# Both ends of a two-layer graph network: denominators in place, other PSUM banks for the last steps, other times and places for the side work

## The chip, the cores and the metric

One core of one Trainium2 chip at a time: the first four experiments (head only, tail only, checks early, all three repairs) ran on one chip and the other seven on another, each group beside its own runs of the kernel before. The engines go by the profile's names: PE is TensorE, DVE VectorE, ACT ScalarE, POOL GpSimd, SP SyncE, which sends most of the DMAs here. PSUM, where TensorE's results land, is shared out in named tiles (`s`, `x`, `qz`, `po`, `pd`). The metric is the device time of one execution in microseconds (us), as the median of several runs. All runs told of here are of the fast state (granted clock 0.993 to 0.996 over the span in the profiled runs), so they can be compared with each other. Of the kernel before, 130 runs were made beside the experiments, and they lie between 3556.3 and 3564.1 us: a difference of 1 us means nothing unless many runs carry it.

## The reference, cut to what matters

```python
# layer 0: pre-norm attention with 8 heads and an adjacency mask; x is 32 x 512 x 512
h = maximum(layernorm(x), 0)
scores = q @ k.T / sqrt(64) + (1 - adj) * -1e9          # q, k, v = h @ Wq, h @ Wk, h @ Wv
x = x + softmax(scores) @ v @ Wo + bo
# layer 1: graph attention
h = maximum(layernorm(x), 0)
hw = h @ W;  s1, s2 = hw @ a1, hw @ a2
att = softmax(leaky_relu(s1[:, None] + s2[None, :]) * adj)
x = x + elu(att @ hw + beta * hw)
```

## The kernel before

One step per batch element b (32, with two more to drain the pipeline). A step has four units of two heads each: scores, exponentials, sums over keys (`es`), denominators (`pd`), values (`po`). Large products are made of seven pieces (names `x_`, `qz_`, `y_`, with the weight combined beforehand), so that sums of operands, made on DVE and POOL, stand between the products. `hn` is the normed input of layer 1, `at` its unnormalised attention matrix, `as` the sum of its four tiles, `pg` the gather `at @ hn`, `dmax` a check of the diagonal.

The order on each engine is the order of the program, and the program decides it with its own clocks: work that is not urgent is put on a list with a time from which it may start, a time by which it is wanted, and a cost. It is taken up where it fits beside TensorE's next piece.

```python
    def pe(us):
        clock["pe"] += us
        till = clock["pe"] + (1.0 if at_ends[0] else 0.4)
        ...   # of the list: what fits until then, the one wanted soonest first
    def later(key, wait, by, cost, fn):
        now = max(clock["dve"], clock["pe"])
        spare.append((key, now + wait, cost, fn, now + by))
    def need(key):
        ...   # everything under this key, now, in order
```

Side work of the first steps: the dot products of W with a (one row per half of W, sent through DRAM to all partitions), W's own combination on POOL, and four checks of adj (`bad`).

```python
        def dot(g, c, o, ar):
            ...   # one multiply-and-sum over 256 columns on DVE
            if c == C - 1 and o == 1:
                ...
                as_row((wa1_r, wa2_r)[g], wa[:, g, :], f"wa{g}")   # by DMA: 512 scattered words
                if g == 1:
                    combine(nc.gpsimd, w1, aw)                      # five operations on POOL
```

Denominators: normally 1/pd goes from PSUM to SBUF on DVE, through DRAM to all partitions, and POOL multiplies. Only the very last unit did it in place in PSUM:

```python
    def finish(b, j, st):
        need("rd")
        if (b, j) == (B - 1, NP - 1):
            return finish_last(b, j, st)
        ...
        def divide():
            nc.vector.reciprocal(rq, pd)
            then("rd", spread)         # ACT copies and sends, SP fetches, POOL multiplies
```

## Time and profile before

| | before |
|---|---|
| median time | 3560.97 us (3559.75 to 3561.69) |
| TensorE (PE) busy | 3506.1 of 3559.0 us |
| TensorE idle before 200 us | 17.5 us |
| TensorE idle after 3400 us | 33.9 us |

The prediction below shows the stretches and the waits. Here are the stretch it leaves out and the places of TensorE's timeline on which both ends are measured. First the stretch from 200 to 400 us (length, then busy PE, PE's weight loads, DVE, ACT, POOL, each with its count, then clock, DMA share, GB/s), then the timeline (start us, busy us, engine, line, operation, out<-in, shapes, count; in brackets the idle time before it and what ended it).

```profile
200.00:400.00 200.00, 199.35 (x1503) 105.90 (x1500) 153.22 (x227) 78.01 (x125) 76.89 (x60) 1.00 0.13 40
```

```profile
152.50 2.08 PE L558 MATMUL ps<-qT,kT 64*128 64x512 f32 x4 [8.48 <-DVE e L570]
...
191.32 1.95 PE L53 MATMUL x_k<-hT,wk 128*64 128x256 f32 x16
...
219.86 3.70 PE L558 MATMUL ps<-qT,kT 64*128 64x512 f32 x16
...
3428.46 3.70 PE L558 MATMUL ps<-qT,kT 64*128 64x512 f32 x16
...
3478.97 1.18 PE L53 MATMUL pe<-ones,as 128*64 128x64 f32 x16 [1.80 <-DVE x L709]
...
3521.06 15.76 PE L53 MATMUL pg<-at,hn 128*64 128x512 f32 x64 [5.52 <-DVE dmax L827]
```

What the reader is to see: from 220 us on TensorE hardly waits (0.65 us idle between 200 and 400), so what the first steps save or lose arrives at the scores of the last unit (3428.46). In twelve of the thirteen traces of this record these two places lie 3207.8 to 3209.4 us apart; the thirteenth is told below. I therefore measure the head by the start of step 2's first scores (219.86) and the tail by the time from the scores of the last unit to the start of the last gather: 3521.06 - 3428.46 = 92.6 us.

### The profile page before, as it was taken

The page shows a single profiled execution, that of the slowest core. Times are in us where ns is not written, and L with a number is a line of the kernel's source. Part 1 is how long each engine was busy: PE and PEld are TensorE (multiplying, and loading weights), DVE is VectorE, ACT ScalarE, POOL GpSimd, SP SyncE. Part 2 cuts the span into 40 slices and gives each one's busy share as a digit, 9 for nine tenths or more (in the row PEclk, how much of TensorE's full clock was granted, in tenths as well). Part 3 has the DMA queues.
Part 4 walks back from the last instruction along what each step waited for, and adds up shares of the span by engine and source line. Part 5 has one row for each costly group of instructions (what it writes and reads, how often), then busy time and mean ns, then how long its engine had stood idle before and what let it go on. Part 6 is the DMA issues. An engine that isn't in the chain of part 4 may idle for free.

```text
span 3559.0 us, 64141 instructions
## 1 busy us (share of the span) xinstructions
PE 3506.1 (99%) x26353; PEld 1885.4 (53%) x26354; DVE 2727.3 (77%) x4207; ACT 1452.9 (41%) x2310; POOL 1396.6 (39%) x1095
## 2 busy tenths in 40 slices
PE   9899999999999999999999999999999999999987
PEld 5455555555555555555555555555555555555544
DVE  6877777787777777777877777877777877778775
ACT  3244443444343444434444434444344444344432
POOL 5332444333443334443334433344433344333342
PEclk9999999999999999999999999999999999999998
DMA  4001111011111011110111110111110111111110
GB/s 137 19 28 49 49 45 46 26 44 45 52 46 37 28 49 48 48 49 31 34 46 51 45 37 30 46 49 48 48 37 28 45 51 46 37 34 43 48 34 28
DMA packets 109395, 154.76 MB, mean 43 GB/s; under 512 B 16492, under 2 KB 54888, under 8 KB 109096
## 3 DMA queue, kind: packets, MB, share of 16 engines
q1 hardware_dynamic: 106496, 148.22, 13.1%
q8 instruction: 210, 3.44, 0.4%
q10 hardware_dynamic: 2392, 2.10, 0.2%
q14 instruction: 89, 0.73, 0.1%
q0 software_dynamic: 208, 0.27, 0.0%
HBM read 116.40 MB, written 34.14 MB: 42 GB/s over the span
## 4 chain that ended last, share of the span: by engine, by line
PE 94%; DVE 4%; DMA 1%; POOL 0%; issue 0%; ACT 0%; SPq 0%; POOLq 0%; ACTq 0%; DVEq 0%
PE ps L558 12%; PE pg L53 12%; PE po L609 12%; PE qz_k L53 5%; PE qz_q L53 5%; PE qz_v L53 5%; PE qz_w L53 4%; PE qz_y L53 4%; PE x_k L53 3%; PE x_v L53 3%; PE x_q L53 3%; PE y_k L53 3%; PE y_v L53 3%; PE y_q L53 3%; PE x_w L53 3%; PE y_w L53 3%
## 5 line engine op out<-in xcount | busy, mean ns | idle before, releaser
L585 ACT ACTIVATE e<-e 128x1024 f32<-128x1024 f32 x512 | 541.5, 1058 | 212.9 <-DVE e L570 176.8
L648 POOL TENSOR_TENSOR oT<-oT,rd 128x512 f32<-128x512 f32 x127 | 172.6, 1359 | 940.7 <-DMA rd<-rd 737.9
L570 DVE SCALAR_TENSOR_TENSOR e<-maskT,ps 128x1024 f32<-128x1024 uint8 x384 | 456.4, 1216 | 85.4 <-PE ps L558 85.2
L558 PE MATMUL ps<-qT,kT 64*128 64x512 f32 x2048 | 478.1, 604 | 12.7 <-DVE e L570 11.6
L609 PE MATMUL po<-e,v 128*64 128x512 f32 x2048 | 464.1, 594 | 0.0
L53 PE MATMUL pg<-at,hn 128*64 128x512 f32 x2048 | 448.9, 596 | 6.3 <-DVE dmax L827 5.5
L582 DVE TENSOR_TENSOR es<-es,e 128x1024 f32<-128x1024 f32 x254 | 381.8, 1503 | 11.0 <-DVE es L582 0.5
L558 PEld LDWEIGHTS ps<-qT,kT 64*128 64x128 f32 x2048 | 186.0, 186 | 301.5 <-issue 206.5
L501 POOL TENSOR_TENSOR qT<-qT,edge 128x256 f32<-128x256 f32 x128 | 85.3, 689 | 560.5 <-DVE qT L497 560.5
L53 PEld LDWEIGHTS pg<-at,hn 128*64 128x64 f32 x2048 | 145.9, 138 | 294.5 <-issue 289.5
L609 PEld LDWEIGHTS po<-e,v 128*64 128x64 f32 x2048 | 148.6, 137 | 229.8 <-issue 217.9
L861 POOL TENSOR_TENSOR y<-y,x 128x512 f32<-128x512 f32 (+1 forms) x126 | 159.5, 1271 | 186.8 <-DVE y L853 183.7
L688 POOL TENSOR_TENSOR x<-x,c_row 128x512 f32<-128x512 f32 x128 | 193.3, 1530 | 98.9 <-DMA x<-in_x_dram 98.9
L359 DVE TENSOR_SCALAR x<-x,mv,rs 128x512 f32<-128x512 f32 x128 | 103.5, 851 | 158.7 <-POOL rs L334 158.5
L638 DVE RECIPROCAL rd<-pd 128x256 f32<-128x256 f32 x127 | 222.3, 1750 | 2.7 <-POOL oT L648 2.3
L793 ACT ACTIVATE at<-at 128x512 f32<-128x512 f32 x128 | 80.2, 628 | 290.3 <-DVE at L789 286.2
L766 DVE CUSTOM_DVE_ANT_0 scr<-hn,wa_r 128x512 f32<-128x512 f32 x256 | 168.8, 689 | 36.7 <-ACT hn L753 36.7
L582 DVE TENSOR_TENSOR es<-e,e 128x1024 f32<-128x1024 f32 x127 | 189.7, 1494 | 0.9 <-PE pd L629 0.8
L53 PE MATMUL qz_y<-w,vT 128*64 128x256 f32 x1520 | 182.8, 383 | 5.2 <-ACT qz_y L464 3.0
L851 DVE TENSOR_SCALAR y<-y 128x512 f32<-128x512 f32 x128 | 56.2, 439 | 142.3 <-ACT y L848 142.3
L565 DVE SCALAR_TENSOR_TENSOR e<-maskT,ps 128x512 f32<-128x512 uint8 x256 | 163.6, 680 | 0.0
L839 ACT COPY gT<-pg 128x512 f32<-128x512 f32 x128 | 74.9, 586 | 197.8 <-PE pg L53 195.9
(228 smaller groups left out, 6315.0 us busy)
## 6 DMA issues: line engine op xcount, KB each, us to landing
x<-in_x_dram SPq DMA_DIRECT2D x130, 256.0 KB
out_dram<-y SPq DMA_DIRECT2D x128, 256.0 KB
rd<-rd SPq DMA_DIRECT2D x254, 128.0 KB
x<-in_x_dram SPq DMA_DIRECT2D x62, 512.0 KB
s<-row_s SPq DMA_DIRECT2D x32, 256.0 KB
rd<-rd ACTq DMA_DIRECT2D x127, 4.0 KB
adj<-in_adj_dram SPq DMA_DIRECT2D x4, 256.0 KB
wk<-in_L_gnn_Wk_dram ACTq DMA_DIRECT2D x3, 256.0 KB
```

The source lines that it names most:

```text
L53: nc.tensor.matmul(out[s : s + HD], lhsT[:, s : s + HD], rhs, start=start, stop=stop, skip_group_check=onto)
L558: nc.tensor.matmul(ps[s], st["kT"][j][rows, ts(k, P)], st["qT"][j][rows, :], start=True, stop=True)
L565: nc.vector.scalar_tensor_tensor(e[:, s, :], maskT[:, k, :], NEG, ps[s], op0=ALU.mult, op1=ALU.add)
L570: nc.vector.scalar_tensor_tensor(e, maskT[:, k, :].unsqueeze(1).to_broadcast([P, 2, N]), NEG, p, op0=ALU.mult, op1=ALU.add)
L582: (nc.gpsimd if early else nc.vector).tensor_tensor(es, one, e, op=ALU.add)
L585: nc.scalar.activation(e, e, AF.Exp)
L609: nc.tensor.matmul(po[s * HD : (s + 1) * HD, :], v[k // 2][:, k % 2, (2 * j + s) * HD : (2 * j + s + 1) * HD], e[k][:, s, :], start=k == 0 ...
L638: nc.vector.reciprocal(rq, pd)
L648: then("rd", lambda: nc.gpsimd.tensor_tensor(o, o, rd, op=ALU.mult), 6.0)
L688: nc.gpsimd.tensor_tensor(r[:, t, :], r[:, t, :], c_row, op=ALU.add)
L766: nc.vector.tensor_tensor_reduce(scr, st["hn"][t], r, 1.0, 0.0, op0=ALU.mult, op1=ALU.add, accum_out=st["s12"][:, g, t : t + 1],)
L861: (nc.vector if b == B - 2 else nc.gpsimd).tensor_tensor(yu, yu, x_[:, :, ts(i, H)], op=ALU.add)
```

## The change

Its intent: at the head, get DVE's dot products and checks out of the way of the scores (the wait of 8.48 us); at the tail, free PSUM banks and get DVE sooner through its list. Cut to its core:

```diff
-            later("bad", 60.0, 200.0, 1.35, lambda t=t: other(t))
+            later("bad", 120.0, 200.0, 1.35, lambda t=t: other(t))
...
-                    later("wa", 40.0, 75.0, 0.5, ...dot...)
+                    later("wa", 40.0, 50.0, 0.75, ...dot...)
...      # sums: the longer cost for the third unit in the first two steps too
-                    "es", ..., 1.9 if j == 2 and b > 1 else 1.2,
+                    "es", ..., 1.9 if j == 2 else 1.2,
...      # where the dots must be done: second half of the first norm, not the first Wo
         def second():
+            need("wa")
...
         def most_of_w():
-            need("wa")
--- tail
-        if (b, j) == (B - 1, NP - 1):
+        if b == B - 1 and j >= NP - 2:
             return finish_last(b, j, st)
...
-        pd = psum.tile([P, N], F32, name=f"pd_{b}_{j}", tag="pd")
+        pd = psum.tile([P, N], F32, name=f"pd_{b}_{j}", tag=("pd", "po")[j % 2])
...      # the pair of the last Wo
+        return seven(f"w{b}", wo, ..., "s" if b == B - 1 else "qz")
...      # the last diagonal: bank po in place of x, and ahead of the elu
-            "P": most_of_y, "E": lambda: diagonal(b - 1, prev), "S": lambda: z_(b - 2),
+            "P": most_of_y, "E": lambda: diagonal(b - 1, prev, "po"), "S": rest_of_y,
...      # k: the last norm's rest and the reciprocals first
-            B: "0p.qmURzviDlngPES", B + 1: "gJY",
+            B: "k0pq.mURzviDlngPES", B + 1: "gJY",
```

The three numbers of `later` are the wait until the work may start, the time by which it is wanted, and its cost. So the checks may start only from 120 us, while the dots are wanted sooner (50 in place of 75 us) at a higher cost each; what comes later for the dots is the place where they must be done. The expectations below call both "wanted later".

Cut are `rest_of_y` (the order of the held elu blocks: block (1,1), then (0,0), then (0,1)), the helper behind `k`, and a start of 16 in place of 4.5 us for `at` of the last two elements. In the last order string the point (the denominators' step) also moved, to behind `q`.

More of the change, by code (lines that the diff above doesn't have):

```diff
@@ L323, in row_constants @@
                 for o in range(2):
-                    later("wa", 40.0, 75.0, 0.5, lambda g=g, c=c, o=o, ar=ar: dot(g, c, o, ar))
+                    later("wa", 40.0, 50.0, 0.75, lambda g=g, c=c, o=o, ar=ar: dot(g, c, o, ar))
     def stats(src, name, mv):
@@ L429, in turn, with seven @@
         st["h"] = h
-    def seven(name, w, B, tokens, one, two, scale=1.0, more=None):
+    def seven(name, w, B, tokens, one, two, scale=1.0, more=None, pair_="qz"):
         def times(p, a, bl, start, onto=False):
@@ L454, in seven @@
         yield
-        qz = psum.tile([P, 2, N], F32, name=f"qz_{name}", tag="qz")
+        qz = psum.tile([P, 2, N], F32, name=f"qz_{name}", tag=pair_)
         z_ = qz[:, 1, :]
@@ L589, in rest @@
                 held.append(lambda: later(
-                    "es", 2.2 if k < T - 1 and b > 1 else 1.2, gap(b, j) - 6.0 + k, 1.9 if j == 2 and b > 1 else 1.2,
+                    "es", 2.2 if k < T - 1 and b > 1 else 1.2, gap(b, j) - 6.0 + k, 1.9 if j == 2 else 1.2,
                     lambda: total(k, e)
@@ L669, in finish_last @@
         finished.add((b, j))
-        st["largest"] = lambda: nc.scalar.activation(
+        st["largest"].append(lambda: nc.scalar.activation(
             pd, pd, AF.Copy, accum_out=rsum[:, b, j : j + 1]
-        )
+        ))
         for k in range(2):
@@ L728, in more @@
             st["share"] = lambda: share(0)
-        return seven(f"w{b}", wo, st["oT"], True, one, two, 1.0 / VS, more)
+        return seven(f"w{b}", wo, st["oT"], True, one, two, 1.0 / VS, more, "s" if b == B - 1 else "qz")
     def norm1(b, st, rows):
@@ L804, in logits, with diagonal @@
         for k in range(T):
-            later(("at", b), 4.5, 20.0, 1.5, lambda k=k: start(k))
-    def diagonal(b, st):
+            later(("at", b), 4.5 if b < B - 2 else 16.0, 20.0, 1.5, lambda k=k: start(k))
+    def diagonal(b, st, tag="x"):
         need(("hn", b))
         need(("at", b))
-        pd = psum.tile([P, T, HD], F32, name=f"pe_{b}", tag="x")
+        pd = psum.tile([P, T, HD], F32, name=f"pe_{b}", tag=tag)
         for t in range(T):
@@ L868, in one, with add @@
         def one(i, k, p):
-            elu(i, k, p)
+            if b == B - 2 and i == 0:
+                st["elu"] = [lambda: elu(i, k, p)]
+            else:
+                elu(i, k, p)
         def two(i, k, p, q):
+            if b == B - 2:
+                st["elu"].append(lambda: add(i, k, p, q))
+            else:
+                add(i, k, p, q)
+        def add(i, k, p, q):
             s = p if i == 0 else wtile([P, N], f"yq_{b}_{i}_{k}", "y", 3)
@@ L885, in new_state @@
             "x": load(b), "e": [[] for _ in range(NP)], "es": {}, "o": [], "x1": [], "at": [], "g": [],
-            "dots": 0,
+            "dots": 0, "largest": [],
         }
@@ L951, in most_of_y, with rest_of_y, last_sums_behind @@
                 next(old["pieces"])
+        def rest_of_y():
+            block0, *others = old["elu"]
+            others[0]()
+            block0()
+            others[1]()
+            z_(b - 2)
+        def last_sums_behind():
+            while any(e[0] == ("hn", b - 2) for e in spare):
+                run_spare(next(i for i, e in enumerate(spare) if e[0] == ("hn", b - 2)))
+            run_all("rd")
         def X():
@@ L1014, in step @@
             "Q": lambda: run(proj_q(b + 1, nxt)),
-            "p": lambda: first_y(b - 3), "q": lambda: more_y(b - 3), "v": lambda: prev["largest"](),
-            "m": lambda: run_all(("hn", b - 2)),
+            "p": lambda: first_y(b - 3), "q": lambda: more_y(b - 3), "v": lambda: [f() for f in prev["largest"]],
+            "m": lambda: run_all(("hn", b - 2)), "k": last_sums_behind,
             "i": most_of_w, "l": lambda: run(prev["pieces"]),
-            "P": most_of_y, "E": lambda: diagonal(b - 1, prev), "S": lambda: z_(b - 2),
+            "P": most_of_y, "E": lambda: diagonal(b - 1, prev, "po"), "S": rest_of_y,
             "f": lambda: residual(b, cur, 0, "x", 4),
```

## The prediction

> **What bounds the kernel now.** I read the page's busy line first, then the stretches of 200 us, then the waits of TensorE (PE) alone, then the timelines of all engines at both ends.
>
> ```profile
> PE 3506.1 (99%) x26353; PEld 1885.4 (53%) x26354; DVE 2727.3 (77%) x4207; ACT 1452.9 (41%) x2310; POOL 1396.6 (39%) x1095
> ...
> 0.00:200.00 200.00, 182.54 (x1443) 104.09 (x1446) 155.96 (x222) 72.32 (x108) 91.43 (x80) 0.97 0.25 76
> ...
> 400.00:600.00 200.00, 200.00 (x1500) 107.07 (x1498) 150.58 (x242) 84.12 (x136) 74.93 (x59) 1.00 0.11 37
> ...
> 3400.00:3600.00 200.00, 125.10 (x848) 64.30 (x844) 100.33 (x185) 46.76 (x83) 57.31 (x48) 0.92 0.08 26
> ```
> The columns of a stretch are its length, then busy PE, weight loads, DVE, ACT, POOL, then clock and DMA. PE is idle 3559.0 - 3506.1 = 52.9 us in all: 17.5 before 200 us and 33.9 of the last 159. The middle is PE without gaps, so a change at the ends can win some 50 us at the very most, 1.4%.
>
> ```profile
> PE ps L558 <- DVE e L570: 11.6, 6, 8.5
> PE qz_w L53 <- DVE y L853: 5.8, 1, 5.8
> PE pg L53 <- DVE dmax L827: 5.5, 1, 5.5
> PE qz_y L53 <- ACT qz_y L464: 3.0, 1, 3.0
> PE pe L53 <- DVE y L853: 2.8, 1, 2.8
> PE qz_w L53 <- ACT qz_w L464: 2.4, 1, 2.4
> PE pd L658 <- ACT pd L644: 2.2, 1, 2.2
> PE qz_y L53 <- DVE yq L874: 2.1, 1, 2.1
> PE pe L53 <- DVE x L709: 1.8, 1, 1.8
> ```
> These are the waits (total us, times, longest) that the change aims at. The 8.5 is one wait at 144 us: the scores' PSUM pair cannot be refilled while DVE works through eleven dots of W with a. From the row "PE qz_w <- DVE y" on, all but the 2.4 lie after 3436 us.
>
> ```profile
> 3447.19 1.22 DVE L748 SCALAR_TENSOR_TENSOR nb<-mv,rs 128x2 f32<-128x2 f32 x1 [3.71 <-POOL rs L334]
> ...
> 3466.36 0.77 DVE L786 SCALAR_TENSOR_TENSOR at<-s,s,adjT 128x512 f32<-128x512 f32 x1
> ...
> 3519.28 1.50 DVE L819 SCALAR_TENSOR_TENSOR at<-ident,bd,at 128x128 f32<-128x128 f32 x4
> ```
> In the timeline of DVE (start, us, idle before it in brackets) from 3434 to 3480 there is one gap worth the name, these 3.71 us: POOL stood with the product of unit 2, waiting for reciprocals to return by DMA, and the 0.7 us power behind it held DVE. So most PE waits at the end are DVE's order, not missing PSUM: what counts there is how much earlier DVE gets through its list.
>
> **What the Trainium skill says.** "TensorE: Matmul & The Clock Gate", What's actually happening: after about 3.4 us of idle window the array runs at half rate until it has again been busy that long. The trace agrees roughly: after the 8.48 us wait four score matmuls took 2.08 us instead of 1.13, and a piece of sixteen that takes 1.73 took 3.68 for 16 after the 5.75 us wait; the clock of 150 to 160 us was 0.71. "SBUF — State Buffer", Who interferes with whom: a DVE operation with two SBUF inputs and a POOL operation that reads SBUF block each other. The trace agrees: the dots took 1.40 us each while POOL was busy and 0.34 when it was not. "DMA: Bandwidth & Descriptors", Queues, rings and completion order: a semaphore increment lands only after every earlier write of that DMA engine, across queues. The trace fits: the row of W·a (512 scattered words) took 10.87 us from issue to release, and the reciprocals' row, sent by ACT at 163.33, released SP only at 169.2. "VectorE: DVE Perf Modes", First, the fixed hardware budget, says that reciprocal iterates; here 128x256 take 1.75 us against 0.69 for a 128x512 product.
>
> **The tail, part by part.** (a) Unit 2's sums in place: one reciprocal of 1.75 becomes two, and a product of 0.69 moves from POOL to DVE: +2.44 on DVE. Against it go the gap of 3.71, the stretched 1.22 us operation behind it (-1.1) and 0.28 of gap at the reciprocal between the dots. (b) The new order on DVE starts with statistics and both nb at 3434.2 to 3436.2, then reciprocals to 3439.6, the product to 3440.3, three sums of 1.22 to 3444.0 (about 0.9 more as POOL's vT falls beside them), eight dots of 0.615 to 3449.8, reciprocals and product to 3453.9. Before, that point was 3455.1: 1.2 gained, and I allow 1.5. (c) PE's wait for the pd bank disappears, but pd_3 now waits for the sums: about 2.3 to 3 us in place of 2.24. The 3.0 for ACT goes, as nb_0 is early, yet PE then waits for yq at 3455 to 3456, some 5 us: DVE is the bound. (d) Last Wo in the scores' banks: the 5.75 wait disappears, Wo's second piece comes 6 us earlier, the third waits for ACT's copy to about 3465. But the next PE instruction that matters, the diagonal of 30, waits for DVE's at and x adds (11.6 us of DVE after the elu). That is moved only by the 1.5 of (b). Most of the 5.75 turns up there again.
> (e) The last diagonal. Before: as ready at 3509.94, then DVE elu work to 3519.03, diagonal to 3521.06, then the gather. After: PE's pe runs as soon as as is there (1.2), DVE's diagonal 2.0, so 3513.2; but the gather's first bank, x, still holds elu block (0,0), now after block (1,1): yq 0.65, exponentials 0.95, 0.44 + 0.88 + 0.67 for (1,1), 0.44 + 0.88 for (0,0) = 4.9 with gaps, so 3518.3. That is 2.7 gained of the 5.5, as the wait passes from dmax to the x bank. Sum: 1.5 + 2.7 = 4.2, plus some 0.6 since the gather (15.76 us against 13.95 of the one at 245 us) starts less cold. Tail: 4.8 gained. From the gather's start to the end nothing changes.
>
> **The head.** (f) Removed: 8.48 + 2.35 (copy behind the reciprocal) + 0.56 (the bad checks before step 1) + about 1.6 (two smaller waits), and some 3 us of slow matmuls: 16. Four dots now precede the scores of unit 1, seven follow, and POOL is idle there, as the combine of W has moved behind a later product. So at the end of the transposes (183.75 before) PE should be some 11.5 us early. (g) That is given back in three places, seen in the order of instructions. First, rd_0's reciprocal is now behind all of e_2, so the bank of pd_1 is free only at 168.2 when PE is there at 164: 4.2 (already in the 11.5). Second, POOL has the product with rd_0, then W's combine (five operations, 5.7), then the power, then tT: the product waits for reciprocals by DMA, queued just behind the second row of W·a. If that row takes 8.4 us as the first did, POOL starts at about 177, t1 is ready at 187.6, and PE, through with x_k at 180.5, waits 7 us (only 3 if the row does not hold it). Third, the four bad checks (1.4 each) stand between the dots and the sums: from the last kT to the qT that frees z DVE has 3.7 + 5.8 + 3.6 + 1.75 + 0.8 + 1.4 + 0.8 = 17.8, plus 0.8 for kT itself, PE 12.7 of work: 5.9 of wait. Two cold starts cost 1.5 each (estimate, from the 1.7 to 2.0 us of the slow pieces above). From the end of x_k, which was at 193.3 and would now be at 180.5: 12.8 - 7.1 - 1.5 - 5.9 - 1.5 = -3.2. Head: -3, with 4 either way.
> Sum: 4.8 - 3 = 1.8. I lean a little further to a gain, because my chains take every order at its worst: 3.5 us from 3561 gives 3557.5.
>
> **The rivals.** First, *the head keeps its gain*: the combine falls in a gap, the checks run while PE still has projections; then head +8, tail +5: 3548. For it: the 8.48 is one clear wait. Against it: POOL and DVE both work in order, and PE had no slack at 190 to 217 us in the trace. Second, *the tail gives nothing*: POOL operations beside DVE stretch the sums and at by a few us (at L789 0.69 to 1.65 in the trace), head -3: 3564. Third, *all targeted waits vanish*: 8.5 + 5.8 + 5.5 + 3 + 2.8 + 2.4 + 2.2 with their cold matmuls, about 35: 3526. Against it: DVE's list from 3434 to 3480 is full, and the waits hang in one chain.
>
> **Range and chances.** 3557.5 us, with 3549 to 3565 for 8 in 10: the head's three give-backs carry most of the spread. Two per cent would be 71 us, more than PE's whole idle time, so a gain above 2% is out, and a loss needs a stall that nothing shows: 0.005, 0.985, 0.01.
>
> **What would show it.** Right: the 8.5 at 144 us gone, in its place waits for pd_1 (ACT pd, about 4), qz_k (POOL tT, 3 to 7) and qz_q (DVE qT, about 6) between 160 and 220 us; step 2's first scores at 217 to 224 us, against 219.86; in the tail no wait of qz_w for y, a larger wait at pe of 30, the gather of 31 waiting for y L854 in place of dmax, and the last 38 us as before. Wrong: if step 2's scores come before 213 us (the give-backs were not there), or if the gather of 31 starts less than 2 or more than 8 us earlier relative to the start of the last step.

## The result, and the profile after

| | before | after |
|---|---|---|
| median time | 3560.97 us | 3561.17 us (3559.06 to 3564.23) |
| ratio, fast runs of the same rounds | 1 | 1.0002, 95% interval 0.9984 to 1.0019 |
| step 2's first scores | 219.86 | 224.80 |
| scores of the last unit | 3428.46 | 3434.01 |
| last gather, counted from there | 92.6 | 89.3 |

A ratio is always the mean time of one kernel's fast runs over that of the other's of the same rounds, so it is not quite the ratio of the medians. The time did not change: 3557.5 had been predicted, with 3549 to 3565 as the range. Below the sum it is not quiet: the head lost 5 us and the tail won 3 to 4. Busy line, stretches and the waits of TensorE of the kernel after:

```profile
PE 3507.7 (98%) x26349; PEld 1887.9 (53%) x26350; DVE 2719.2 (76%) x4209; ACT 1453.1 (41%) x2310; POOL 1390.3 (39%) x1094
```

```profile
0.00:200.00 200.00, 186.36 (x1483) 108.06 (x1484) 141.40 (x211) 73.01 (x109) 86.69 (x81) 0.97 0.23 76
200.00:400.00 200.00, 191.94 (x1414) 100.22 (x1408) 155.82 (x234) 77.56 (x125) 70.73 (x57) 0.98 0.12 39
...
3400.00:3600.00 200.00, 130.35 (x870) 67.13 (x866) 107.16 (x189) 48.09 (x86) 62.93 (x51) 0.92 0.08 25
```

```profile
PE qz_q L53 <- ACT qz_q L464: 6.8, 1, 6.8
...
PE pe L53 <- DVE x L709: 5.1, 1, 5.1
PE qz_k L53 <- POOL hT L379: 4.9, 1, 4.9
PE pd L629 <- ACT pd L644: 4.4, 1, 4.4
...
PE pg L53 <- DVE y L854: 0.8, 1, 0.8
```

TensorE's idle time went down by 3.8 us before 200 us and up by 7.4 between 200 and 400 us: the 8.5 at 144 us is gone, and three waits (4.4, 4.9, 6.8) stand in its place further on. The 5.8 of Wo and the 5.5 of the gather are gone too; the first is largely back as 5.1 at the diagonal of element 30. The places in TensorE's timeline that answer to those of before:

```profile
187.47 3.57 PE L53 MATMUL qz_k<-hT,wk 128*64 128x256 f32 x16 [4.86 <-POOL hT L379]
...
214.06 3.68 PE L53 MATMUL qz_q<-tT,wq 128*64 128x256 f32 x16 [6.75 <-ACT qz_q L464]
...
224.80 3.70 PE L558 MATMUL ps<-qT,kT 64*128 64x512 f32 x16
...
3483.79 1.22 PE L53 MATMUL pe<-ones,as 128*64 128x64 f32 x16 [5.08 <-DVE x L709]
...
3523.35 14.24 PE L53 MATMUL pg<-at,hn 128*64 128x512 f32 x64 [0.78 <-DVE y L854]
```

The waits of qz_k and qz_q cost more than themselves: the piece behind each takes 3.6 us, where the pieces of a running stream start every 1.73 us. Why POOL is late, from SP's list and POOL's timeline:

```profile
168.50 0.37 SPq L137 DMA_DIRECT2D row_wa<-wa  x1
169.72 1.09 SPq L647 DMA_DIRECT2D rd<-rd  x2
176.76 0.33 SPq L138 DMA_DIRECT2D wa_r<-row_wa  x1
```

```profile
177.26 1.27 POOL L648 TENSOR_TENSOR oT<-oT,rd 128x512 f32<-128x512 f32 x1 [25.50 <-DMA rd<-rd]
178.49 1.28 POOL L281 TENSOR_TENSOR w<-a_w,w 128x512 f32<-128x512 f32 x1
...
186.16 1.26 POOL L379 TENSOR_TENSOR hT<-hT 128x512 f32<-128x512 f32 x1
```

The reciprocals of unit (0,0) are fetched at 169.72, 1.2 us behind the scattered row of W·a, and released with it, at 177. Then POOL combines W, which nobody wants yet, before it makes the operand on which TensorE waits. And why the last one is late, from DVE's and ACT's timelines:

```profile
207.96 0.69 DVE L255 TENSOR_REDUCE bad<-sq 128x1 f32<-128x512 f32 x1
...
210.96 1.75 DVE L638 RECIPROCAL rd<-pd 128x256 f32<-128x256 f32 x1
```

```profile
212.80 0.39 ACT L644 ACTIVATE pd<-rd 128x256 f32<-128x256 f32 x1 [8.30 <-DVE rd L638]
...
213.43 0.57 ACT L464 COPY qz_q<-y_q 128x512 f32<-128x512 f32 x1
```

The four checks run as one block from 203.29 to 208.56 on DVE, the reciprocal of unit 2 stands behind them, ACT's copy of it behind that, and only then comes the copy for which TensorE waits. In the kernel before, ACT made its copy of the reciprocal at 208.5, and TensorE did not wait.

### The profile page after: what moved, and what is told of

It is laid out like the page before. It is cut to its first block, busy times and chain, and to the rows that moved or that the text cites. A ratio compares the mean times of both kernels' runs of the same rounds, so it can differ in the third digit from the quotient of the medians.

```text
span 3561.3 us, 64126 instructions
## 1 busy us (share of the span) xinstructions
PE 3507.7 (98%) x26349; PEld 1887.9 (53%) x26350; DVE 2719.2 (76%) x4209; ACT 1453.1 (41%) x2310; POOL 1390.3 (39%) x1094
## 4 chain that ended last, share of the span: by engine, by line
PE 94%; DVE 3%; DMA 1%; POOL 1%; issue 1%; ACT 0%; SPq 0%; ACTq 0%; POOLq 0%; DVEq 0%
PE ps L558 12%; PE po L609 12%; PE pg L53 12%; PE qz_k L53 5%; PE qz_q L53 5%; PE qz_v L53 5%; PE qz_w L53 5%; PE qz_y L53 4%; PE x_v L53 3%; PE x_k L53 3%; PE x_w L53 3%; PE y_k L53 3%; PE y_v L53 3%; PE y_q L53 3%; PE x_q L53 3%; PE y_w L53 3%
## 5 line engine op out<-in xcount | busy, mean ns | idle before, releaser
L582 DVE TENSOR_TENSOR es<-es,e 128x1024 f32<-128x1024 f32 x254 | 382.1, 1504 | 10.5
L688 POOL TENSOR_TENSOR x<-x,c_row 128x512 f32<-128x512 f32 x128 | 182.7, 1448 | 102.2 <-DMA x<-in_x_dram 102.2
```

Source lines behind the costliest of these rows:

```text
L582: (nc.gpsimd if early else nc.vector).tensor_tensor(es, one, e, op=ALU.add)
L688: nc.gpsimd.tensor_tensor(r[:, t, :], r[:, t, :], c_row, op=ALU.add)
```

## The experiments

The ratios are against the kernel before, of the same rounds. "Step 2" is the start of its first scores; "gather" is the last one's start, counted from the scores of the last unit.

| kernel | ratio | 95% interval | median us | step 2 | gather |
|---|---|---|---|---|---|
| before | 1 | | 3560 to 3563 | 219.86 | 92.6 |
| after | 1.0002 | 0.9984, 1.0019 | 3561.17 | 224.80 | 89.3 |
| head only | 1.0012 | 1.0006, 1.0019 | 3566.60 | 225.94 | 91.6 |
| tail only | 0.9988 | 0.9982, 0.9995 | 3558.92 | 222.59 | 89.4 |
| after, checks early | 0.9975 | 0.9965, 0.9986 | 3553.72 | 217.41 | 88.0 |
| after, combination later | 0.9987 | 0.9980, 0.9993 | 3555.47 | 219.21 | 89.1 |
| after, reciprocal early | 0.9985 | 0.9978, 0.9992 | 3554.99 | 216.41 | 89.4 |
| after, checks and reciprocal | 0.9977 | 0.9968, 0.9987 | 3551.46 | 212.27 | 89.5 |
| after, all three | 0.9935 | 0.9921, 0.9948 | 3539.59 | 203.46 | 88.6 |
| all three, old Wo banks | 0.9940 | 0.9927, 0.9954 | 3538.47 | 204.02 | 89.2 |
| tail, old Wo banks | 0.9988 | 0.9982, 0.9995 | 3555.69 | 219.78 | 88.0 |
| tail, old diagonal | 1.0003 | 0.9994, 1.0012 | 3561.13 | 220.55 | 92.0 |
| tail, unit 2 the old way | 0.9989 | 0.9981, 0.9998 | 3556.31 | 218.62 | 90.4 |

The median of before was 3562.74 beside head only, tail only, checks early and all three repairs, 3560.09 beside combination later, reciprocal early, old Wo banks with the tail alone and old diagonal, and 3559.75 beside the last three, so medians of different groups are not compared with each other, ratios are. In the last column kernels with the same tail (after, tail only, and the five repaired heads with the tail as it is in after) lie between 88.0 and 89.5: differences under 1.5 us in it are not read. In the column of step 2 the five kernels with the head of before lie between 218.62 and 222.59: a single trace places the head to within 4 us, and what is read there is which waits are in it.

### The head alone

The first five places of the diff, up to the mark "tail", put into the kernel before.

> The kernel before with only the changes of its first three steps (dots and bad checks wanted later, W wanted at the second half of the first norm, longer sums reserved for). My theory: the two ends are independent, since TensorE has no gap between 250 and 3400 us, so this kernel shows the head's part of the change alone: first scores of step 2 at 224.8 us as in the kernel after (219.86 before), waits of pd_1 4.4, qz_k 4.9 and qz_q 6.8 us in it, the scores of unit (31,3) some 5 us later than before, and the time 4 to 6 us longer than the kernel before (about 3566). Rival: the whole change does nothing at either end that a run can show, and the 5 us of the two traces is a difference from run to run: then the time is within 1.5 us of before.

The ratio of 1.0012 is 4.3 us, inside the expectation, and the interval leaves out 1. In the trace step 2 begins at 225.94, the three waits are 4.4, 5.3 and 7.0, and the last unit's scores start at 3434.52. The head's part of the change is a loss.

### The tail alone

The kernel after with those five places as before.

> The kernel after with its head as before: only the tail's parts. My theory: the tail gains what the trace of after shows relative to the first scores of unit (31,3): the last gather ends 4.8 us earlier, 1.5 of that is lost at the very end, so 3.3 us shorter than before (3556.5 to 3558.5), and the scores of unit (31,3) start at 3428.5 as before. Rival 1: the 1.5 lost at the end is chance, then 4.8 shorter. Rival 2: nothing is gained, then within 1 us of before.

The ratio of 0.9988 is 4.3 us won, so the two halves cancel: +4.3 - 4.3 = 0, and after is at 1.0002. That lies between the expectation (3.3) and its first rival (4.8), and the interval covers both. One number missed: the last unit's scores started at 3431.20, not 3428.5. In this trace the head was 1.3 us later from the start (142.49 against 141.17) and waited for the scores' bank 3.45 us once more at 181.55, with the same program: the head of the kernel before is not the same to the microsecond from run to run.

### First repair: the checks early again

```diff
-            later("bad", 120.0, 200.0, 1.35, lambda t=t: other(t))
+            later("bad", 60.0, 200.0, 1.35, lambda t=t: other(t))
```

> The kernel after with only the four late bad checks wanted as early as before (from 60 instead of 120 us). My theory: the checks' 5.3 us burst at 203 to 208.6 us ahead of the last sums and of the reciprocal is what makes ACT's copy for qz_q late, so the wait of 6.75 us for qz_q goes down to under 1.5 us and its piece runs warm (1.7 to 1.9 us instead of 3.68); against that up to 1 us more early on: step 2's first scores at 217 to 219 us instead of 224.8, and 5 to 8 us shorter than the kernel after. Rival: DVE is the bound of the whole stretch (the checks cost it 5.3 us wherever they stand), so that an earlier wait grows instead and the gain is under 2 us.

TensorE's timeline of this kernel, where the wait of qz_k is still there and step 2 begins:

```profile
187.91 3.68 PE L53 MATMUL qz_k<-hT,wk 128*64 128x256 f32 x16 [5.76 <-POOL hT L379]
...
217.41 4.05 PE L558 MATMUL ps<-qT,kT 64*128 64x512 f32 x16
```

The qz_q wait has vanished altogether, and step 2 comes 7.4 us earlier than in after; 6.75 for the wait and 1.9 for the slow piece had been there to win. By the ratios it is 9.6 us under after, more than the 5 to 8 expected, though the interval of after alone is 12 us wide. The rival is out: DVE has room for 5.3 us of checks, but not at 203 us.

### Second repair: W's combination later

```diff
-                if g == 1:
-                    combine(nc.gpsimd, w1, aw)
...
         def H_():
             nxt["hT"] = combos(b + 1, "tT", nxt["h"])
+            if b == 1:
+                need("wa")
+                combine(nc.gpsimd, w1, aw)
```

> The kernel after with only one thing moved: W's five combining operations on POOL come behind the combination for tT instead of ahead of it. My theory: POOL has tT ready about 5.7 us earlier (by 182 instead of 187.5), so the wait of qz_k for POOL (4.9) and its slow piece (3.57 instead of 1.75) go; DVE had idled 3.0 us for POOL's power at that place and gets only those 3, so the wait of qz_q grows from 6.8 to some 8 to 10: step 2's first scores at 219 to 222 us against 224.8 after, and 3 to 6 us shorter than after. Rival 1: the qz_q wait takes all of it (DVE is the bound from 160 to 215 us): no change in time. Rival 2: no take-over at all: 6.7 shorter, 218.

The wait of 4.9 is gone (1.0 is left further on, for DVE), and step 2 comes 5.6 us earlier. My detail was wrong: the qz_q wait did not grow, it stayed at 6.7. DVE's wait for POOL's power is still there (4.59 in place of 3.03 us, at 190.97 and 190.79). What went are two waits behind it in the trace of after: 1.53 us for ACT's normed input, which stood behind ACT's copy of the late qz_k, and 3.17 us for a later qz_k piece itself. DVE had been held by TensorE's own lateness, so both moved together: the checks began at 198.3 in place of 203.3.

### Third repair: the reciprocal of unit (0,0) ahead of the dots

```diff
         def most_of_w():
+            for i in [i for i, e in enumerate(spare) if b == 1 and e[0] == "rd"][:1]:
+                run_spare(i)
             fourth(b - 1, "uT", prev["oT"])
```

> The kernel after with only the reciprocal of unit (0,0) put ahead of the dots on DVE. My theory: the bank of pd_1 is free in time, so the wait of 4.4 and the slow transposes (3.68 instead of 2.0) go; the reciprocals' DMA goes out some 15 us earlier, POOL multiplies at about 163 instead of 177, has W combined before tT is wanted, and the qz_k wait of 4.9 with its slow piece goes too: TensorE is 12 us earlier at the end of x_k. The late checks still stand ahead of the sums on DVE, so qz_q still waits, 6 to 10 us: step 2's first scores at 211 to 216 us, 9 to 13 us shorter than after. Rival: the qz_k wait stays as POOL's combine is what costs, then only about 6 shorter (219).

The pd_1 wait and the qz_k wait are both gone, as the theory has it. But step 2 came at 216.41, just outside 211 to 216, and the ratio of 0.9985 is 6 us under after, not 9 to 13. The reason is a line of DVE's timeline that I had not foreseen, and TensorE's wait behind it:

```profile
194.03 0.69 DVE L767 CUSTOM_DVE_ANT_0 scr<-hn,wa_r 128x512 f32<-128x512 f32 x1 [5.52 <-DMA wa_r<-row_wa]
```

```profile
208.66 3.68 PE L53 MATMUL qz_q<-tT,wq 128*64 128x256 f32 x16 [9.02 <-DVE qT L497]
```

With the reciprocal in front, the last dots fell behind the next unit's work, so the second row of W·a left at 180.3 in place of 168.5, and the products with that row had to wait for it.

### Two repairs without the combination, and all three

> The kernel after with two of the three repairs: checks early and the reciprocal ahead of the dots, W's combination on POOL left where it was. Question: are the three give-backs independent sums, or does one repair stand in for another? My theory: with the reciprocal early, POOL has tT before W's combination anyway, so no qz_k wait; but in the order of instructions the last dots stand behind the next unit's work again, so the second row of W.a leaves only at about 180 us and DVE waits for it (5.5 us in the run with the reciprocal alone), and qz_q waits 2 to 5 us: step 2's first scores at 208 to 213 us (203.5 with all three), time 4 to 10 us longer than with all three. Rival: the combination's place does nothing once the reciprocal is early: 203 to 205, as with all three.

> The kernel after with all three give-backs taken out: checks early, the combination of W on POOL behind the combination for tT, the reciprocal of unit (0,0) ahead of the dots. My theory: the waits of pd_1 (4.4), qz_k (4.9) and qz_q (6.8) and two slow pieces (1.8 each) go, so step 2's first scores come at 206 to 212 us against 224.8 after and 219.86 before, and the time is 12 to 18 us under that of after and 8 to 13 under that of before (3548 to 3553). Rival: the head is bound by DVE's or POOL's whole list, so other waits take their place (at qz_x, at the first norm, or at the first Wo) and no more than 5 us are won against after.

With checks and reciprocal alone step 2 begins at 212.27, inside the expectation; DVE waits 6.2 us for the row of W·a and TensorE 4.4 at qz_q. The time is 15 us above that of all three (0.0042 of 3560), more than the 4 to 10 expected, as the lateness goes on past step 2 (this is the thirteenth trace: 3212.2 us from there to the last unit's scores):

```profile
231.22 1.17 PE L53 MATMUL pe<-ones,as 128*64 128x64 f32 x16 [2.44 <-DVE as L801]
```

The values behind that wait took 5.30 us in place of 3.61, so some 4 us more were lost there. What separates the two kernels is not where POOL combines W: with two repairs it does so after the operands of qz_k anyway (from 175.97, from 174.61 with all three). It is the `need("wa")` that came with the third repair: it has the last dots done ahead of that place, so that with all three the second row leaves at 167.52 in place of 181.50. How much of the 15 us the combination's place carries was not tested apart from it, and the traces give no sign of any. With all three, the three waits are gone and none takes their place between 170 and 400 us:

```profile
203.46 3.70 PE L556 MATMUL ps<-qT,kT 64*128 64x512 f32 x16
```

That is 21.3 us before the kernel after. The three waits (4.41 + 4.86 + 6.75 = 16.0) and the slow pieces behind them (about 1.6 + 1.8 + 1.9, against pieces of the same shape at full rate) make 21.3, so no new wait has to be assumed, as far as a scatter of 4 us between traces lets one say so. Both parts of my expectation were too low: step 2 at 206 to 212, and 12 to 18 us under after (24 by the ratios) or 8 to 13 under before (23). The waits and two slow pieces that it named add up to 19.7 on their own. The medians say the same: 3539.59 beside 3562.74 of before, 0.65% faster. This kernel beats both.

### The tail's parts

The last Wo's pair back in its old banks, the rest of the tail as in tail only:

```diff
-        return seven(..., "s" if b == B - 1 else "qz")
+        return seven(..., "qz")
```

> The tail-only kernel with the last Wo's pair back in its old PSUM banks; the order of instructions on every engine is the same as in the tail-only kernel. My theory (step d of the prediction): the wait of qz_w for an elu operation, about 5.8 us, is back, but the diagonal of 30 comes at the same time, since DVE's at and x adds set it (its own wait shrinks from 3.4 to about 1): the last gather starts within 0.5 us of the tail-only kernel's, counted from the scores of unit (31,3) (89.4), and the time is within 1 us of it. Rival: the bank was worth its 5.8 us, so the gather starts 4 to 6 us later and the time is 4 to 6 us longer.

```profile
3466.34 2.61 PE L53 MATMUL qz_w<-wo,uT 128*64 128x256 f32 x16 [4.07 <-DVE y L853]
...
3478.72 1.18 PE L53 MATMUL pe<-ones,as 128*64 128x64 f32 x16 [1.83 <-DVE x L709]
```

The wait for the elu is back (4.1, with one of 5.8 expected), the wait at the diagonal shrinks from 3.4 to 1.8, and the diagonal stands 49.76 us behind the last unit's scores against 49.77 with the new banks. The ratio is the same, 0.9988. So the new banks moved a wait and won nothing that can be seen. The trace had the gather 1.5 us earlier without them; the same edit on top of the three repairs tested that:

> All three repairs, and the last Wo's pair back in its old banks. My theory: the banks of the last Wo are worth nothing (run with the tail alone: gather 1.5 us earlier without them in the trace, the same time), so the time is that of the kernel with three repairs within 1.5 us, 0.993 to 0.994 of before. Rival: the 1.5 of the trace is real, then 1 to 2 us shorter (0.9930).

It had the gather 0.65 us later and the ratio at 0.9940 against 0.9935 (1.8 us, with intervals that overlap). The 1.5 was scatter, and its place is known: the Wo piece behind the diagonal took 3.66 us in the trace of tail only and 1.93 in that with the old banks.

The last diagonal and the elu as before, the rest of the tail as in tail only:

```diff
-            ..., "E": lambda: diagonal(b - 1, prev, "po"), "S": rest_of_y,
+            ..., "E": lambda: diagonal(b - 1, prev), "S": lambda: z_(b - 2),
```

> The tail-only kernel with the last diagonal back behind the elu and in its old bank, and the elu blocks in their old order. My theory (step e): the wait of the last gather for dmax, about 5.5 us, is back in place of the 0.6 for y, the gather starts 2.7 to 3.3 us later counted from the scores of unit (31,3) (about 92.4 against 89.4) and takes 15.8 instead of 14.2: 3 to 4.5 us longer than the tail-only kernel, so all of the tail's gain is in this part. Rival: the gain comes from the denominators in place (step b), then no more than 1 us longer.

```profile
3520.44 15.31 PE L53 MATMUL pg<-at,hn 128*64 128x512 f32 x64 [6.36 <-DVE dmax L827]
```

The wait for dmax is back, the gather is 2.5 us later than in tail only and takes 1.1 us longer, and the ratio is 1.0003 against 0.9988, 5 us where 3 to 4.5 were expected. In the trace 1.8 more was lost behind the gather, where an output block left late (told below). All that the runs can see of the tail's gain is in this part.

Unit 2's denominators the old way and without the work moved ahead:

```diff
-        if b == B - 1 and j >= NP - 2:
+        if (b, j) == (B - 1, NP - 1):
...
-            B: "k0pq.mURzviDlngPES"
+            B: "0pq.mURzviDlngPES"
```

> The tail-only kernel with unit 2's denominators finished the old way, and the last sums no longer run ahead. My theory (steps a to c, corrected by the run with the old diagonal, which was 0.6 us ahead of the kernel before at the last gather): DVE's new order ahead of the diagonal of 30 is worth 0.6 to 1.5 us, so the last gather starts 90 to 91 us after the scores of unit (31,3), against 89.4 of the tail-only kernel; the waits of pd_3 for ACT (2.2) and of qz_y for ACT (3.0) are back; time 0 to 1.5 us longer. Rival: the order is worth the 3.7 us gap of DVE that it closes: 3 to 4 us longer.

(The bank of pd_3 went back as well, and `m` again stands where it stood: the order was "0p.qm".) The waits of pd_3 (2.2) and qz_y (3.3) for ACT are back, the gather is 1.0 us later, and the ratio is 0.9989. The part is worth 0 to 1 us. The later start of `at` for the last two elements was not tested alone.

## Why the prediction was right or wrong

The time lies 3.7 us above the number given, in a range of 16 us that holds gains and losses alike; what tests the working are the places in the trace.

**What bounds the kernel: right.** The middle has no gap, so the ends simply add: head +4.3, tail -4.3.

**Head, "-3, with 4 either way": right, the mechanism in each place, the sizes nearly.** The early gain at the end of the transposes was 10.5 us (173.20 against 183.75), predicted 11.5. Of the three places that give it back, pd_1 waited 4.41 (4.2). For qz_k the prediction had POOL at 177 and the operand at 187.6, and they came at 177.26 and 187.4; its wait was 4.86 in place of 7, since TensorE was through with x_k at 182.6 and not 180.5: the term "12.8" in its sum should have been 10.65. Most of that is a slip in the sum, as its own early gain of 11.5 would have put the end of x_k at 181.8. That the row holds the reciprocals fits this trace, as they reach POOL 0.5 us after the row is in. But the evidence that the prediction gave for it does not show it: in the kernel before, SP's fetch at 169.2 stood behind SP's own wait for the row in program order. For qz_q it named DVE's qT and 5.9; the profile names ACT's copy and 6.75. The checks on DVE are the cause all the same (with them early the wait is gone), but the last link goes over the reciprocal of unit 2 and ACT's list. Slow pieces cost 1.6 to 1.9 each (1.5). With the measured terms the sum is 10.65 - 4.86 - 1.8 - 6.75 - 1.9 = -4.7, and the trace has -4.94. The check "step 2 at 217 to 224" missed by 0.8.

**Tail, "4.8 gained": about right in sum, not by its parts.** The run of the tail alone has 4.3 by its ratio. Counted to the last gather's start in the trace, 3.3 us were won, 4.2 predicted, so some of the agreement in the sum is luck. Step (b), 1.5 from DVE's order, is the term that failed: DVE was through with the product of unit 3 only 0.7 us sooner (25.9 us after the last unit's scores against 26.6; 1.2 worked out), and the last `as` was ready 81.0 us after the last unit's scores against 81.5, so 0.45, less than the scatter of that column, and undoing that part changed the gather by 1.0 and the time by nothing that can be seen. Step (e) held: from `as` to the gather 8.3 us against 11.1, 2.8 won where 2.7 was predicted, and without it the gain is gone. Step (c) had the right waits with other sizes: pd_3 3.6 for the sums (2.3 to 3) and qz_y 3.3 for yq (some 5). Step (d) held: most of the wait of Wo reappeared at the diagonal of 30 (5.1 against 1.8). The signs named for the tail came as well: no wait of qz_w for y, and the gather waits for y L854.

**"From the gather's start to the end nothing changes": right as a number, wrong as a statement.** It was 37.9 us in both. But the gather took 14.24 in place of 15.76, as less of it ran at the slow rate (0.6 predicted), and the end gave it back. This is in the chain of waits of the kernel after:

```profile
3548.22 3.66 DMA out_dram<-y
```

An exponential of the last elu blocks waits for an output block to leave its buffer. In the tail-only trace, with the same code there, that block was away in time, and the same stretch was 36.7 us. The other traces bear this out. With the tail's order of the elu, from the end of the last gather to the end of the program it is 22.2 to 22.5 us in the five traces where the block is not in that chain, 22.5 and 22.7 where it stands there with 2.4 us, 23.1 with 3.0, 23.7 with 3.7 (after) and 23.9 with 3.8. So it moves a run by up to 1.7 us. The runs of after lie at 3559 and at 3563 to 3564; this alone is too small for that, and what splits them stays open.

**The lean to 3.5: wrong.** The sum of the working was 1.8 and the measured one is 0. "My chains take every order at its worst" was not so: both halves came out slightly worse than worked out.

**What the prediction did not ask:** whether the three give-backs could be had without the head's gain. As I read the program, all three are accidents of order in a list (a check that may not start early, a reciprocal that is too long to fit where shorter dots do, a combination tied to the last dot), and putting them right, with the last dots brought forward by the third repair, turns the head's loss of 4.3 us into a gain of 16 to 19 (219.86 - 203.46 in the traces; 0.9988 - 0.9935 in the ratios).

## What to carry to other kernels

Where several engines work in order, removing a wait in one place sends the work that caused it somewhere else: look up where it lands, and what stands behind it there on every engine. A part whose gain is zero can hide two parts of opposite sign; run the halves before giving either up. Work that nobody wants yet costs nothing in a gap, and its full length, with a slow piece on top, when it stands just ahead of something on the chain.

## What the Trainium skill lacked or had wrong

- "DMA: Bandwidth & Descriptors", Anatomy of one DMA, puts the fixed part of a DMA (there on the GpSimd path) at about 2 us and calls the generation of descriptors small. It has no number for a row of single words: here 512 scattered words, 2 KB, took 8.4, 10.9 and 8.3 us from SP's issue to the release of the DMA that waits for them (8.2 to 10.1 in the traces with repairs). A fetch behind such a row is late: the reciprocals' fetch let POOL go after 7.5 us when issued 1.2 us behind such a row (169.72 to 177.26), after 11.8 when 0.6 us behind it (151.23 to 163.04, with all three repairs), and after 3.6 with no row ahead (188.50 to 192.06, with the combination later). Whether that is the order of semaphores that the prediction cites from this page or the row's words standing ahead on the same SP queue, no run here separates.
- "TensorE: Matmul & The Clock Gate", Why this matters for your kernels, has as its rule no gaps over about 3 us. The runs show slow pieces after less: 3.46 us for sixteen matmuls after a wait of 2.85 us, with only 1.2 us of work between it and an earlier wait of 1.35; and 2.83 us after a single wait of 2.35 (before, at 165.11; the granted clock was 0.51 from 166 to 168 us). They also show that one and the same wait of 3.62 us left the four matmuls behind it at 1.98 us and the next piece at 2.54 (after), or at 1.08 and 1.93 with no slow piece at all (all three repairs). That spread fits the page's free-running window.
- No page says how much the landing of one and the same store varies from run to run: one output block held the chain for 3.66 us in the trace of after, which cost that run some 1.3 us, and was no wait at all in the tail-only trace. Over the traces with this tail it cost 0 to 1.7 us.
